# State-space stage of a decoder layer: the states of all pairs as one stream, four engines in program order

## The chip, the cores and the metric

The kernel runs on one core of a Trainium2 chip. The time is device microseconds of one execution. The core's engines work side by side: PE (TensorE, matmuls, with its weight loads as PEld), DVE (VectorE), ACT (ScalarE), POOL (GpSimd) and SP (SyncE, which here only starts transfers). Each works through its own queue in order and waits on semaphores for the others.

## The reference, cut to what matters

A decoder layer on x of shape 8 x 256 x 128: a state-space (Mamba-like) block, a cross attention to a context, and six layers of windowed attention and gated feed-forward. Only the first is concerned. For D = 256 channels, N = 16 states and 4 convolution taps it computes:

```python
Xn = layernorm(X)
X_main = silu(causal_conv(Xn @ W_up1))                  # 256 channels
delta, Bm, Cm = split(X_main @ W_ll + b_ll)             # 256, 16, 16; softplus on delta
A_bar = exp(delta * A)                                  # per channel and state
U = X_main * (A_bar - 1) / (delta * A) * (delta * Bm)
H = A_bar[t] * H + U[t]                                 # scan over t
Y[t] = sum over n of Cm[t, n] * H[:, n]
out = X + (Y * silu(Xn @ W_up2)) @ W_down
```

Since (A_bar − 1) / (delta A) × delta Bm = (A_bar − 1) Bm / A, the kernel keeps w = X_main Bm / A and scans m = (m + dw) × A_bar with dw the difference of w in time; the rest of H is w itself, and its share of Y comes from one product over all states (`s_ps`, `xs`).

## The kernel before, in words

Two sequences make a pair; there are four pairs. Channels lie on partitions in two halves `h` of 128, the 512 columns are the pair's tokens. A unit is one state `n` of one half:

- VectorE: `wz` = xm × (1/A) × the broadcast row of B (L542), then two scans `m`, one per sequence (L523);
- POOL: `dw` = the time difference of `wz` (L548), and `mc` = m × the broadcast row of C (L525);
- ACT: `ab` = exp(A × dt) into PSUM (L98 is the line of a helper that many activations share);
- PE: the add of `mc` into `y` in PSUM with an identity matrix (L503);
- SP: per state two transfers `rows` of 256 KB that spread a row of B and one of C over the partitions (L537), read back from `bc_dram`, which ACT's queue wrote (L402).

Buffers: `rows` 4, `wz` 4, `dw` 3, `m` 2, `mc` 6, `ab` 2, and two small PSUM banks under the tag `s` that nearly every matmul other than `y` goes through. The scan of a unit is written two units behind its `wz`.

`scan` runs the 16 states of a pair. Between states it advances two generators by one step or two: `post`, which ends the pair before (gate `yg`, down projection `dn_ps`, layer norm, `x1`), and `pre`, which prepares the next pair (load and turn the tokens, statistics `bn_st` and `bn_mv`, turn again, `conv`, the activation into `xm`, the product `bc_ps` for B and C, `dt` by a softplus, and the gates). `xm` is copied to PSUM (`xm_ps`, L511) for states 2 and later; the first two states read `xm` itself. `y` is begun after state 2 by `s_ps` and `xs` (L556 to L559), and the adds begin at state 4. Beside pair 2 and in pair 3, `project` makes the first pair's queries, keys and values for the cross attention; for pair 0 it goes through the small banks, each half of an accumulator left by ACT at once.

The order: up to the first pair's `dt`, PE, ACT and VectorE run as written (`manual_schedule`). From there to the end of the stage a scheduler chooses each engine's order among what the program's steps offer, by estimated costs. A few edges hold it: `behind_exps` puts some ACT work behind the last `ab`, and `with_table` puts exponentials and logarithms behind the load of their activation table. The later stages are not touched, except that `project` for later pairs is written without its case for the first.

Of the kernel before, what the change touches and what calls it, by code (L numbers as in the profile page):

```python
# [9 lines left out]
FP = mybir.dt.float32  # L10
# [4 lines left out]
P = 128  # L15
B, S, D = 8, 256, 128
NPAIR = B // 2
TP = 2 * S
# [31 lines left out]
def decoder_kernel(ctx: ExitStack, tc: tile.TileContext, a: dict, out: bass.AP):  # L50
# [163 lines left out]

    def project(p, got):
# [23 lines left out]
        got.update(qT=qT, kT=kT, v=v)  # L239
        for j in range(NHB // 2):  # L240
            for dst, w, src, q in ((qT, wq, la, True), (kT, wkv, cn, False)):
                pr = ps_big("pr") if big else None
                for i in range(2):
                    c = 2 * j + i
                    o = pr[:, i * TP : (i + 1) * TP] if big else ps_s("pr")
                    T.matmul(  # L246
                        o, lhsT=w[:, c * P : (c + 1) * P], rhs=src, start=True, stop=True
                    )
                    if not big:
                        A.activation(dst[:, c, :], o, AF.Copy, scale=HD**-0.5 if q else 1.0)  # L250
                d2 = dst[:, 2 * j : 2 * j + 2, :].rearrange("p c t -> p (c t)")
                if big and q:
                    A.activation(d2, pr, AF.Copy, scale=HD**-0.5)
                elif big:
                    V.tensor_copy(d2, pr)
                yield
        for j in range(4):
            pr = ps_big("pv") if big else None
            for i in range(2):
                at = slice(i * 512, (i + 1) * 512)  # L260
                o = pr[:, at] if big else ps_s("pv")
                T.matmul(
                    o, lhsT=cn[:, j * P : (j + 1) * P],
                    rhs=wkv[:, INNER + i * 512 : INNER + (i + 1) * 512], start=True, stop=True,
                )
                if not big:
                    A.copy(v[:, j, at], o)
            if big:
                A.copy(v[:, j, :], pr)
            yield  # L270


    with (
# [80 lines left out]
        def pre(p, got, t_in=None):  # L354
# [49 lines left out]
            got.update(bc=bc, cb=cb, b_ps=[])  # L404
# [26 lines left out]
            def minus_bc():  # L431

                c_ps = ps_s("c_ps")
                T.matmul(
                    c_ps[:NS], lhsT=ident[: 2 * NS, NS : 2 * NS], rhs=bc_sb, start=True, stop=True
                )
                V.scalar_tensor_tensor(cb, c_ps[:NS], -1.0, bc_sb[:NS], ALU.mult, ALU.mult)

            if p:
                minus_bc()  # L440
                for h in range(2):
                    d_ps = step_of(h)
                    yield
                    softplus(h, d_ps)
                yield
            else:

                for h in range(2):
                    d_ps = step_of(h)
                    t = ps1.tile([P, TP], FP, tag="ab", name="b_ps")  # L450
                    T.matmul(
                        t, lhsT=ident[: 2 * NS, h : h + 1].to_broadcast([2 * NS, P]), rhs=bc_sb,
                        start=True, stop=True,
                    )
                    got["b_ps"].append(t)
                    softplus(h, d_ps)
                yield
                minus_bc()
            g_ps = []
            for h in range(2):  # L460
                g_ps.append(ps_s("g_ps"))
                T.matmul(
                    g_ps[h], lhsT=w_up2[:, h * P : (h + 1) * P], rhs=xn, start=True, stop=True
                )
            yield
            load_table("exp_and_others")
            for h in range(2):
                g = sp.tile([P, TP], FP, tag=f"gate{h}", name="gate")
                with behind_exps():
                    with_table(A.activation, g, g_ps[h], AF.Tanh)  # L470
                V.scalar_tensor_tensor(g, g, 1.0, g_ps[h], ALU.add, ALU.mult)
                gate.append(g)
            load_table()
# [21 lines left out]
        def scan(p, x, xm, gate, dt, bc, b_ps, cb, steps, spare):  # L495


            y = [ps_o("y0"), ps_o("y1")]
            late = []

            def add_up():
                for h, n, mc in late:
                    T.matmul(y[h], lhsT=ident, rhs=mc, start=False, stop=(n == NS - 1))  # L503
                late.clear()

            xp1 = []
            for h in range(2):
                t = ps1.tile([P, TP], FP, tag=f"xm{h}", name="xm_ps", bufs=1)  # L510
                A.copy(t, xm[h])  # L511
                xp1.append(t)

            def scan_of(h, n, dw, rows):
                c = h * NS + n
                ab = ps1.tile([P, TP], FP, tag="ab", name="ab")
                exps.append(
                    with_table(A.activation, ab, dt[h], AF.Exp, scale=aa[:, c : c + 1])
                )
                m = sp.tile([P, TP], FP, name="m")  # L520
                for b in range(2):
                    t = slice(b * S, (b + 1) * S)
                    V.tensor_tensor_scan(m[:, t], dw[:, t], ab[:, t], 0.0, ALU.add, ALU.mult)  # L523
                mc = sp.tile([P, TP], FP, name="mc", bufs=6)
                G.tensor_tensor(mc, m, rows[:, 1, :], ALU.mult)  # L525
                late.append((h, n, mc))

            waiting = []
            for n in range(NS):
                if n > 3:  # L530
                    add_up()

                rows = sp.tile([P, 2, TP], FP, name="rows", bufs=4)
                early = n < len(b_ps)
                for i in range(1 if early else 0, 2):
                    r = i * NS + n
                    nc.sync.dma_start(out=rows[:, i, :], in_=bc[r : r + 1, :].to_broadcast([P, TP]))  # L537
                for h in range(2):
                    c = h * NS + n
                    w = wzs.pop(0)  # L540
                    wzs.append(w)
                    V.scalar_tensor_tensor(  # L542
                        w[:, :, 1:], two((xm if n < 2 else xp1)[h]), ia[:, c : c + 1],
                        two(b_ps[n] if early else rows[:, 0, :]),
                        ALU.mult, ALU.mult,
                    )
                    dw = sp.tile([P, TP], FP, name="dw", bufs=3)
                    G.tensor_tensor(two(dw), w[:, :, 1:], w[:, :, :S], ALU.subtract)  # L548
                    waiting.append((h, n, dw, rows))

                    if len(waiting) > 2:
                        scan_of(*waiting.pop(0))
                if n == 2:
                    for h in range(2):
                        s_ps = ps_s("s_ps")
                        T.matmul(s_ps, lhsT=iaT[:, h, :], rhs=cb, start=True, stop=True)  # L556
                        t = sp.tile([P, TP], FP, tag=f"yg{h}", name="xs1")
                        V.tensor_tensor(t, xm[h], s_ps, ALU.mult)
                        T.matmul(y[h], lhsT=ident, rhs=t, start=True, stop=False)  # L559
                for _ in range(0 if n == 0 else 2 if n <= 5 or p == NPAIR - 1 else 1):  # L560
                    next(steps, None)
                if n > 5:
                    next(spare, None)
            for args in waiting:
                scan_of(*args)
            add_up()
            for _ in steps:
                pass
            return y

        def both(*gens):

            gens = list(gens)
            while gens:
                for g in list(gens):
                    try:
                        next(g)
                    except StopIteration:
                        gens.remove(g)
                        continue  # L580
                    yield

        nxt = {}
        last = pre(0, nxt, t_in0)
        engines = {mybir.EngineType.PE, mybir.EngineType.Activation, mybir.EngineType.DVE}
# [9 lines left out]
        turn_decay()  # L595
        for p in range(NPAIR):
            cur, nxt = nxt, {}
            if p == 1:
                load2()
            if p == NPAIR - 2:  # L600
                beside = project(0, first)
            ahead = pre(p + 1, nxt) if p + 1 < NPAIR else beside
            y = scan(p, **cur, steps=both(last, ahead), spare=beside if p == NPAIR - 2 else iter(()))
            last = post(p, cur["x"], cur["gate"], y)
# [671 lines left out]
```

## Time and profile before

| what | value |
|---|---|
| runs | 2251.42, 2255.55, 2256.18 us; median 2255.55 |
| profiled execution | 2257.74 us, of which the span on the core is 2255.9 |
| state-space stage | first `dw` at 28.2 us, last `mc` ends at 375.2 |
| cross attention and the six layers | from about 376 us to the end |
| busy in the whole span | PE 2100.3, DVE 1734.9, ACT 1430.0, POOL 1637.5 us |

Busy time by stretch, from the windows view (us busy, instructions in brackets, granted TensorE clock as a share of full speed); the four stretches are roughly the four pairs:

| stretch, us | PE | DVE | ACT | POOL | clock |
|---|---|---|---|---|---|
| 28 to 110 | 63.95 (118) | 66.44 (113) | 44.28 (69) | 68.82 (62) | 0.82 |
| 110 to 185 | 57.15 (126) | 65.49 (112) | 35.77 (56) | 67.75 (60) | 0.83 |
| 185 to 275 | 69.61 (146) | 76.06 (124) | 46.79 (75) | 76.37 (67) | 0.81 |
| 275 to 376 | 80.42 (160) | 75.79 (118) | 40.91 (67) | 83.46 (74) | 0.88 |

In a line of the groups stand the source line, the engine, the operation, output <- inputs with shapes, the count, then busy us and mean ns of one, then the idle time of that engine just before these instructions and who ended it. In a line of a timeline stand start and duration in us, and in brackets the idle time before it and who ended it; neighbours of the same kind are merged into one line (x2, x4). Durations in the timeline overlap by some 0.05 us, so what an instruction costs its engine is read from start to start. The ends of matmuls are modelled; a 128x512 matmul in float32 shows as two instructions.

### The profile page before, as it was taken

The page shows a single profiled execution, that of the slowest core. Times are in us where ns is not written, and L with a number is a line of the kernel's source. Part 1 is how long each engine was busy: PE and PEld are TensorE (multiplying, and loading weights), DVE is VectorE, ACT ScalarE, POOL GpSimd, SP SyncE. Part 2 cuts the span into 40 slices and gives each one's busy share as a digit, 9 for nine tenths or more (in the row PEclk, how much of TensorE's full clock was granted, in tenths as well). Part 3 has the DMA queues.
Part 4 walks back from the last instruction along what each step waited for, and adds up shares of the span by engine and source line. Part 5 has one row for each costly group of instructions (what it writes and reads, how often), then busy time and mean ns, then how long its engine had stood idle before and what let it go on. Part 6 is the DMA issues. An engine that isn't in the chain of part 4 may idle for free.

```text
span 2255.9 us, 77045 instructions
## 1 busy us (share of the span) xinstructions
PE 2100.3 (93%) x32482; PEld 1314.6 (58%) x32482; DVE 1734.9 (77%) x2533; ACT 1430.0 (63%) x2438; POOL 1637.5 (73%) x1440
## 2 busy tenths in 40 slices
PE   7877888999988999999999999999999999999986
PEld 3232333444444776666767667676776767667653
DVE  6798876444366988888898888888888888888852
ACT  5544544555455777777667777777766677777644
POOL 4888887222267988888888888888888888888740
PEclk8887989999999999999999999999999999999998
DMA  4443331000203444434443434444443434333330
GB/s 138 97 105 95 98 94 47 6 5 1 64 25 58 71 71 85 76 71 78 75 86 70 77 67 87 76 77 70 76 85 68 78 66 83 68 67 65 62 58 10
DMA packets 438326, 155.41 MB, mean 69 GB/s; under 512 B 401886, under 2 KB 418140, under 8 KB 437852
## 3 DMA queue, kind: packets, MB, share of 16 engines
q1 hardware_dynamic: 437500, 150.10, 34.1%
q8 instruction: 255, 4.18, 0.8%
q14 instruction: 91, 0.75, 0.1%
q10 hardware_dynamic: 480, 0.38, 0.1%
HBM read 54.68 MB, written 1.31 MB: 25 GB/s over the span
## 4 chain that ended last, share of the span: by engine, by line
PE 70%; DVE 7%; ACT 6%; POOL 2%; issue 2%; DMA 0%; DVEq 0%; POOLq 0%; ACTq 0%
PE qk_ps L686 13%; PE y_ps L863 7%; PE qkT_ps L742 7%; PE o_ps L849 7%; PE f_ps L933 6%; PE v_ps L686 6%; PE s_ps L790 5%; PE pT_ps L832 3%; PE f_ps L961 3%; PE pr L246 3%; PE o_ps L1107 2%; PE s_ps L1088 2%; ACT ln_sq L98 1%; PE y_ps L1145 1%; DVE rb L704 1%
## 5 line engine op out<-in xcount | busy, mean ns | idle before, releaser
L707 POOL TENSOR_TENSOR qk<-qk,rb 128x512 f32<-128x512 f32 x384 | 481.0, 1274 | 48.4 <-DVE rb L704 29.6
L735 POOL TENSOR_TENSOR qk<-qk,rn 128x1024 f32<-128x1024 f32 x192 | 365.5, 1904 | 12.4 <-ACT rn L98 12.3
L686 PE MATMUL qk_ps<-wqkv,xs 128*128 128x512 f32 x768 | 363.9, 596 | 2.4 <-ACT kz L752 1.4
L812 POOL TENSOR_TENSOR pw<-pw,mx 128x512 f32<-128x512 f32 x192 | 202.0, 1052 | 168.1 <-DVE mx L811 167.9
L709 ACT ACTIVATE sq<-qk_ps 128x1024 f32<-128x1024 f32 x192 | 196.9, 1026 | 165.7 <-PE o_ps L849 123.1
L703 DVE TENSOR_TENSOR qk<-qk_ps,tab 128x1024 f32<-128x1024 f32 x192 | 228.8, 1192 | 67.1 <-PE qk_ps L686 66.2
L704 DVE TENSOR_TENSOR rb<-qk_ps,tab 128x1024 f32<-128x1024 f32 x192 | 233.1, 1214 | 0.0
L716 DVE TENSOR_REDUCE ss<-sq 128x16 f32<-128x1024 f32 x192 | 229.1, 1193 | 5.1 <-ACT sq L709 5.0
L825 POOL TENSOR_TENSOR pw<-pw,mx 128x512 f32<-128x512 f32 x192 | 200.4, 1044 | 39.2 <-ACT fxn L920 32.0
L1097 POOL TENSOR_TENSOR ws<-w 128x512 f32<-128x512 f32 x64 | 81.5, 1273 | 195.7 <-ACT w L98 152.7
L863 PEld LDWEIGHTS y_ps<-oT,wo 128*128 128x128 f32 x1536 | 186.2, 192 | 46.6 <-issue 33.5
L742 PE MATMUL qkT_ps<-ident,qk 128*128 128x128 f32 x1536 | 209.5, 279 | 4.0 <-POOL qk L735 2.9
L525 POOL TENSOR_TENSOR mc<-m,rows 128x512 f32<-128x512 f32 x128 | 163.1, 1278 | 40.2 <-PE y L503 20.4
L863 PE MATMUL y_ps<-oT,wo 128*128 128x128 f32 x1536 | 187.5, 275 | 1.9 <-ACT pT L836 1.6
L857 DVE STREAM_TRANSPOSE oT<-o_ps 128x512 f32<-128x512 f32 x192 | 126.1, 695 | 82.0 <-PE o_ps L849 82.0
L686 PEld LDWEIGHTS qk_ps<-wqkv,xs 128*128 128x128 f32 x768 | 131.3, 191 | 97.5 <-issue 93.0
L523 DVE TENSOR_TENSOR_SCAN m<-dw,ab 128x256 f32<-128x256 f32 x256 | 159.8, 668 | 31.6 <-POOL mc L525 29.8
L790 PEld LDWEIGHTS s_ps<-kz,qT 64*32 64x32 f32 x12288 | 137.8, 105 | 76.1 <-issue 38.6
L686 PE MATMUL v_ps<-wqkv,xs 128*128 128x512 f32 x384 | 180.6, 592 | 0.3 <-ACT sq L709 0.3
L742 PEld LDWEIGHTS qkT_ps<-ident,qk 128*128 128x128 f32 x1536 | 165.2, 141 | 23.8 <-POOL qk L735 3.8
L98 ACT ACTIVATE ab<-dt,aa 128x512 f32<-128x512 f32 x128 | 87.6, 689 | 139.9 <-DVE m L523 136.5
L849 PE MATMUL o_ps<-vz,pT 64*32 64x64 f32 x12288 | 168.6, 225 | 2.3 <-issue 2.3
(187 smaller groups left out, 4146.7 us busy)
## 6 DMA issues: line engine op xcount, KB each, us to landing
vz<-v SPq DMA_DIRECT2D x1152, 64.0 KB, 2.2
rows<-bc_dram SPq DMA_DIRECT2D x126, 256.0 KB, 4.2
vz<-v SPq DMA_DIRECT2D x576, 32.0 KB, 2.0
wqkv<-in_L_ffn_Wqkv SPq DMA_DIRECT2D x18, 512.0 KB, 4.7
wo<-in_L_ffn_Wo SPq DMA_DIRECT2D x48, 64.0 KB, 2.4
w<-in_L_ffn_W SPq DMA_DIRECT2D x6, 341.0 KB, 3.4
t_in<-in_x SPq DMA_DIRECT2D x4, 256.0 KB, 3.4
wkv<-in_L_xattn_Wkv SPq DMA_DIRECT2D x1, 1024.0 KB, 8.0
```

The costliest lines, as they stand in the source:

```text
L686: T.matmul(pr[:, i * 512 : (i + 1) * 512], lhsT=got[n]["xs"][:, tb * P : (tb + 1) * P], rhs=thirds[seq[n][0], c][:, i * 512 : (i + 1) * 51 ...
L703: V.tensor_tensor(t, p3, cs, ALU.mult)
L704: V.tensor_tensor(rb, p3, sn, ALU.mult)
L707: G.tensor_tensor(t[:, :, o], t[:, :, o], rb[:, :, f], ALU.add)
L716: V.tensor_reduce(got[n]["ss"][:, 2 * c + tb, :], got[n]["sq"], AX.X, ALU.add)
L735: G.tensor_tensor(t, t, r, ALU.mult)
L742: T.transpose(t_ps[:, hb * P : (hb + 1) * P], t[:, 2 * hb : 2 * hb + 2, :].rearrange("p h d -> p (h d)"), ident,)
L790: T.matmul(s_ps[i * W : (i + 1) * W, e, c : c + 2 * W], lhsT=qT[r, 4 * g + i, j * W : (j + 1) * W], rhs=kz[r, 4 * g + i, k0 : k0 + 2 * W], ...
L812: G.tensor_tensor(pw, pw, mx[:, 0].unsqueeze(3).to_broadcast([P, 4, 2, 2 * W]), ALU.subtract)
L825: G.tensor_tensor(pw, pw, mx[:, 1].unsqueeze(3).to_broadcast([P, 4, 2, 2 * W]), ALU.mult)
L849: T.matmul(o_ps[i * W : (i + 1) * W, e, c : c + HD], lhsT=pT[r, j, i * W : (i + 1) * W], rhs=vz[r, j, i, :], start=True, stop=True, tile_p ...
L863: T.matmul(y_ps[:, :P], lhsT=wts[d][0][:, hb, :], rhs=got[n]["oT", wh][:, hb // 4, (hb // 2) % 2, :].rearrange("p (w h q) -> p h w q", w=4 ...
```

## The change

Program order now holds for PE, ACT, VectorE and POOL through the whole stage (`manual_schedule` over the four pairs, POOL added). The generators are gone. The states of all pairs form one stream: the units that wait for their scan, and the products that wait for their add, are carried over the border from one pair to the next. After each state `n` of pair `p`, `ended(p - 1, n)` does one step of ending the pair before (states 1 to 5) and `prepare(p + 1, n)` one step of the next pair's preparation (states 1 to 15). Gates and `dt` of a pair are complete before its first state; for pair 0 the gates come after states 1 to 3. `y` of a pair is begun in `ended` at state 2 (`start_y`), for pair 0 after state 1, and adds that have no `y` yet wait in a list. `ab` of the units that still wait is made ahead (`decay_of`). The next pair's activation table is changed once for `xm` and gates together (loads at states 7 and 12). `project` for the first pair is a function of its own: three matmuls a state, each left by ACT, and all of it beside pair 3.

The core of the diff (shortened; repeated parts of unchanged operations are left out):

```diff
+    def project_first(la, cn, qT, kT, v):
...
+        for i, (dst, w, src, scale) in enumerate(work):
+            if i % 3 == 0:
+                while out:
+                    leave()
+            if len(out) == 2:
+                leave()
+            o = ps_s("pr")
+            T.matmul(o, lhsT=w, rhs=src, start=True, stop=True)
+            out.append((dst, o, scale))
+            if i % 3 == 2:
+                yield
...
+        def prepare(p, c, n):
+            if n == 1:
+                c["t_in"] = load_x(p)
...
+            elif n == 3:
+                c["tp"] = turned_tokens(c["t_in"])
+            elif n == 4:
+                A.copy(c["x"], c["tp"])
...
+                for j in range(4):
+                    V.bn_stats(st[:, j, :], c["t_in"][:, j, :])
+                    V.bn_aggr(mv[:, j, :], st[:, j, :])
+            elif n == 5:
+                inv_root(rs, mv[:, :, 1], eps_t)
+                V.scalar_tensor_tensor(mv[:, :, 0], mv[:, :, 0], -1.0, rs, ALU.mult, ALU.mult)
...
+                c["tp"] = turned_tokens(t)
+            elif n == 6:
+                A.activation(xn, two(c["tp"]), AF.Identity, bias=col("ssm_b"), scale=col("ssm_g"))
+                c["acc"] = [ps_s("conv") for h in range(2)]
...
+            elif n in (7, 8, 9):
...
+            elif n == 10:
...
+            elif n == 11:
+                gate_tanhs(c)
+            elif n == 12:
+                gates(c)
+                load_table()
...
+                c["c_ps"] = minus_bc(c)
+                c["d_ps"] = dt_product(c, 0)
+            elif n == 13:
+                stored_bc(c, c["c_ps"])
+                c["ze"] = softplus(0, c["d_ps"])
+                c["d_ps"] = dt_product(c, 1)
+            elif n == 14:
+                dt_sum(c, 0)
+                c["ze"] = softplus(1, c["d_ps"])
+            elif n == 15:
+                dt_sum(c, 1)
...
+        def ended(p, c, n):
+            if n == 1:
...
+            elif n == 2:
+                A.activation(c["r"], c["dn"], AF.Identity, bias=col("ssm_bd"))
+                start_y(pairs[p + 1])
+                T.matmul(c["ln"], lhsT=mean_w, rhs=c["r"], start=True, stop=True)
...
+        def scan_next():
+            i = waiting.pop(0)
+            decay_of(i)
...
+        def start_y(c):
+            y = [ps_o("y0"), ps_o("y1")]
+            for h in range(2):
+                s_ps = ps_s("s_ps")
+                T.matmul(s_ps, lhsT=iaT[:, h, :], rhs=c["cb"], start=True, stop=True)
+                t = sp.tile([P, TP], FP, tag=f"yg{h}", name="xs1")
+                V.tensor_tensor(t, c["xm"][h], s_ps, ALU.mult)
+                T.matmul(y[h], lhsT=ident, rhs=t, start=True, stop=False)
+            c["y"] = y
+        def state(p, c, n):
+            add_up()
...
+                if len(waiting) > 2:
+                    scan_next()
+                if p or n > 1:
+                    for i in waiting:
+                        decay_of(i)
+        order1.enter_context(tc.manual_schedule(engines=engines))
         for p in range(NPAIR):
+            for n in range(NS):
+                state(p, c, n)
...
+                if p:
+                    ended(p - 1, pairs[p - 1], n)
+                if p < NPAIR - 1:
+                    prepare(p + 1, pairs[p + 1], n)
+                else:
+                    if n == 0:
+                        beside = project(0, first)
+                    if n == 1 or n > 2:
+                        next(beside, None)
```

## The prediction

> **What bounds the stage now.** The edit stays inside the state-space stage, so I read, in this order, the windows view (where the stage ends), the groups of POOL and VectorE in its window, and POOL's, VectorE's and PE's timelines there. A "unit" is one state of one half of the channels: one `wz`, one `dw`, two scans `m`, one `mc`; 4 pairs have 128.
>
> POOL's two groups over the first 377 us (count, busy us and mean ns, idle before and who ended it):
>
> ```profile
> L525 POOL TENSOR_TENSOR mc<-m,rows 128x512 f32<-128x512 f32 x128 | 163.1, 1278 | 40.2 <-PE y L503 20.4 <-issue 6.6 <-PE s_ps L556 5.3
> L548 POOL TENSOR_TENSOR dw<-wz 128x512 f32<-128x512 f32 x128 | 136.3, 1067 | 35.2 <-DVE wz L542 32.6 <-DVE m L523 2.4
> ```
>
> Every unit costs POOL a `dw` and an `mc`. In the timeline, POOL runs for long stretches without a gap and then stops dead, mostly on PE:
>
> ```profile
> 64.19 1.27 POOL L525 TENSOR_TENSOR mc<-m,rows 128x512 f32<-128x512 f32 x1 [8.29 <-PE y L503]
> ...
> 98.31 1.27 POOL L525 TENSOR_TENSOR mc<-m,rows 128x512 f32<-128x512 f32 x1
> 99.54 1.03 POOL L548 TENSOR_TENSOR dw<-wz 128x512 f32<-128x512 f32 x1
> 100.54 1.26 POOL L525 TENSOR_TENSOR mc<-m,rows 128x512 f32<-128x512 f32 x1
> ...
> 160.63 1.27 POOL L525 TENSOR_TENSOR mc<-m,rows 128x512 f32<-128x512 f32 x1 [3.49 <-PE bc_ps L393]
> ...
> 190.44 1.26 POOL L525 TENSOR_TENSOR mc<-m,rows 128x512 f32<-128x512 f32 x1 [5.08 <-PE s_ps L556]
> ...
> 277.90 1.26 POOL L525 TENSOR_TENSOR mc<-m,rows 128x512 f32<-128x512 f32 x1 [5.82 <-issue]
> ```
>
> and once more, in pair 3:
>
> ```profile
> 317.20 2.49 POOL L525 TENSOR_TENSOR mc<-m,rows 128x512 f32<-128x512 f32 x2 [7.38 <-PE y L503]
> ```
>
> From start to start a unit takes 100.54 − 98.31 = 2.23 us. The first `dw` starts at 28.2, the last `mc` ends at 375.2: 347.0 us. POOL's own work is 128 × 2.23 + 6 `dt` sums × 1.22 (start to start) = 292.8. So 54 us are lost; the five waits above are 30.1 of them, the rest lies in many gaps under 2 us. POOL is the floor, PE's and VectorE's order makes the gaps.
>
> VectorE in a calm stretch, then where `xm` comes from SBUF:
>
> ```profile
> 120.67 0.74 DVE L542 SCALAR_TENSOR_TENSOR wz<-xm_ps,ia,rows 128x512 f32<-128x512 f32 x1
> 121.32 1.25 DVE L523 TENSOR_TENSOR_SCAN m<-dw,ab 128x256 f32<-128x256 f32 x2
> 122.50 0.72 DVE L542 SCALAR_TENSOR_TENSOR wz<-xm_ps,ia,rows 128x512 f32<-128x512 f32 x1
> ```
>
> A unit costs VectorE 122.50 − 120.67 = 1.83 us, so per state (two units) it gains 2 × (2.23 − 1.83) = 0.80 us on POOL. That is what pays for everything else on VectorE.
>
> **The change, part by part.**
>
> *Lost waits.* The next pair's `bc`, `cb`, `dt` and gates are now finished at states 10 to 15 of the pair before, and `y` of a pair starts at its state 2 on PE with the four adds that are due right behind it, not behind a burst of other matmuls. In the built order of the changed kernel POOL alternates `dw`, `mc` across pair borders. I take all five big waits away (30.1 us) and then ask what is late next: VectorE, which now works in program order and waits at the heads of its queue for PE and ACT, with the scans and `wz` behind it, and POOL behind those.
>
> *The cushion.* `m` has two buffers: a scan starts when the `mc` two units back ends. From then POOL has four instructions before it needs the next state's `wz`: 2 × 2.23 = 4.46 us. Off go the scan (1.18), the `wz` (0.65) and some 0.3 for handovers: VectorE may lose 2.3 us at one place before POOL stands. A ledger for pair 1 or 2 starts with 2.3 and gains 0.80 per state.
>
> - States 0 and 1: four `wz` read `xm` and `rows`, both in SBUF. Their group has 17.6 us for 12, mean 1469 ns against 733 with `xm` in PSUM; from 109.69 to 119.48 the four units took 9.8 us, not 4 × 1.83 = 7.3, so 2.5 more. Left: 2.3 − 2.5 + 1.6 = 1.4. POOL's own instructions in that stretch are longer by 1.3 (an `mc` of 1.71 for 1.27, `dw` of 2.48 for two).
> - State 1 to 2: two `yg` (1.2), PE's three `dn`, `s_ps`, then `xs`, `y`, `s_ps`, `xs` in turn. Before, other work stood between. PE at this place is slow in the trace:
>
> ```profile
> 302.21 2.07 PE L556 MATMUL s_ps<-cb,iaT 16*128 16x512 f32 x2 [1.39 <-ACT qT L250]
> 304.21 2.08 PE L559 MATMUL y<-xs,ident 128*128 128x512 f32 x2
> 306.08 1.91 PE L487 MATMUL dn_ps<-yg,w_dn 128*128 128x512 f32 x2
> ...
> 310.57 1.02 PE L488 MATMUL dn_ps<-x,twice 128*128 128x512 f32 x2
> ```
>
>   A 128x512 matmul (two instructions) takes 1.7 to 1.9 us start to start at first and 0.86 some 8 us later. I count from the end of state 1's scans. The first `dn` starts at 0.75, behind one `yg`; with three matmuls at 1.75 and the rest at 0.9 the first `s_ps` ends at 6.9, `xs` at 7.6, `y` and `s_ps` at 9.5, the second `xs` at 10.2. Without all this VectorE would be through state 2 at 2 × 1.83 = 3.6. So 6.6 lost, 0.8 gained, 1.4 in hand: POOL stands 4.4 us. With all at 0.9 it is 2.2, with all at 1.75 it is 6.9; three is what the trace has in the bursts from 211.7 and 302.2 on (three to four).
> - State 3: `ln_xc` 0.6, covered. State 4: four `bn_st` and `bn_mv`, 1.45 (three and four of them took 1.0 from 270.9 on): 0.45 uncovered. State 5: `x` 0.6, then `bn_mv` waits for ACT's two small `ln_rs` behind an `ab` (0.65 + 0.5 + 0.1) and takes 0.6: 1.9, 1.1 uncovered.
> - States 8, 9, 12, 13 (`xm`, gates, `cb`: 3.1) lie in 8 us of gained time: nothing.
>
> Pair 1 or 2: 32 × 2.23 + 2.44 = 73.8, plus 1.3 + 4.4 + 0.45 + 1.1 = 81.1.
> Pair 0 has the `s_ps`/`y` chain at state 1 with no cushion: `cb` 0.6, `s_ps` 1.9, `xs` 0.6, `y` and `s_ps` 3.7, `xs` 0.6 from 33.0 on; the next `dw` at about 41.2 where POOL is idle from 35.5: 5.7. With 2.0 of first gaps as now and 1.3 at states 4 and 5: 82.8.
> Pair 3 runs the first projection instead. State 3 has `ln_xc`, statistics, a wait and four `t_in`: 4.4 − 0.8 = 3.6 uncovered; state 7 waits for two ACT roots behind an `ab` (2.0) and runs `la` twice (0.89 + 1.28): 4.1 − 0.8 − 1.2 in hand = 2.1. With 1.3 + 4.4: 71.4 + 11.4 = 82.8.
>
> Sum: 28.2 + 82.8 + 2 × 81.1 + 82.8 = 356 for the end of the last `mc`, now 375.2: 19 us.
>
> *Moved at no cost, with its cover.* `rows`: a buffer is free at the `mc` four states back; VectorE asks for the next one at the earliest two units and a scan later, 4.46 + 1.18 = 5.6 us, against 4.2 us (3.5 to 5.0) from issue to landing on SP's queue; if SP lets that margin slip, a wait like the 2.40 before the `wz` at 344.09 returns, once per slip. The `bc` store on ACT's queue now has five states before its first reader. ACT loses 6 of the stage's 18 table loads (1283 ns each) and is busy 36 to 47 us a pair: no gain, no loss. PE adds of one state wait behind the 8 `conv`: `mc` has six buffers, 13 us, against at most 12 at the slow rate. In pair 3, ten instructions a state × 0.43 = 4.3 us of 4.46; at the 0.88 clock of that quarter 4.9, up to 3.5 us late at the end of the stage, kept for the range. Behind the stage nothing moves.
>
> **A rule that speaks against it.** `s_ps` has a mean of 1026 ns and `y<-xs` 1100 where 592 is the fast figure, and the granted clock is 0.56 from 200 to 220 us, where PE only adds. "TensorE: Matmul & The Clock Gate" of the Trainium skill (Part 1) says that idling for about 3.4 us halves the clock and about as long of sustained work restores it; a PE that waits in order idles more. By that rule the burst would have two slow matmuls, not three, and the stall above 3.5 instead of 4.4.
>
> **Rivals.**
> 1. *The cushion does not work* (two `m` buffers, and the waits sit exactly where it is spent). Then all of VectorE's other work falls on POOL: `yg`, `xs` and their chain 6.6, `wz` 2.5 and POOL's 1.3, `ln_xc`, statistics, `x`, `bn_mv` 4.0, `xm`, gates, `cb` 3.1: 17.5 a pair, 73.8 + 17.5 = 91.3, four pairs and the start 393: 18 us slower, 2274. It decides from 347.0/4 − 73.2 = 13.5 us a pair on. For it: 44 scan waits for `mc` in the window show how short the leash is. Against: around 125 VectorE takes `xs` and `yg` and POOL goes on.
> 2. *VectorE's extras hide nearly wholly*, PE being busy enough to keep its clock: 28.2 + 292.8 = 321 at best, 54 us faster; half of my stalls gives 338, 37 faster: 2219, range 2201 to 2224. Against: the chain at state 2 is serial whatever the clock.
> 3. *PE becomes the bound.* Pair 1 has 114 long matmul instructions × 0.43 + 2 = 51 us at full clock; at 51/86.8 = 0.59 mean clock it takes as long as now. At 0.55: 93 us, the stage's end at 399, 24 slower, 2280. Clocks of 0.81 to 0.88 per pair speak against.
> 4. *No change beyond 0.2%*: new stalls eat the 54 by chance.
>
> **How the numbers follow.** The profiled execution took 2257.74 us (span 2255.9, 1.8 around it); the median of three runs is 2255.55, 2.2 lower. I forecast the median: 2255.55 − 19 = 2236. Unknowns of the forecast case: PE's rate (3 × 2.2 less or 3 × 2.5 more), pair 0 (3), pair 3 (4), `rows` slips (up to 5 × 2.4), PE's tail 3.5; not all at once: 2224 to 2252. Chances: forecast 0.60, rival 2 0.17, rival 1 0.12, rival 3 0.04, rival 4 0.07. The range takes the forecast case, the slower half of rival 2 and rival 4: 2212 to 2254, leaving out about 0.2. No change means within 0.2%, 4.5 us, about what runs of this kernel can tell (they lie 4.8 apart): faster 0.78, same 0.07, slower 0.15.
>
> **What would show it.** Right: the last `mc` ends near 356; POOL's waits for PE `y` at most a few us; gaps of 2 to 5 us at state 2 of each pair, ended by `wz` or scans, with VectorE's `xs` waiting for `s_ps`; `wz` waits for `rows` under 8 us in all. Wrong: POOL gaps in every state (rival 1), `mc` waiting for PE `y` in mid-pair (rival 3), an end before 340 (rival 2), or a stage behind 376 that is not as long as before.

## The result, and the profile after

| | before | after |
|---|---|---|
| median | 2254.70 us (5 runs, 2251.42 to 2256.18) | 2239.36 us (5 runs, 2236.05 to 2245.17) |
| ratio | | 0.9926, interval 0.9913 to 0.9939 |
| profiled execution, span | 2257.74, 2255.9 us | 2237.36, 2235.6 us |
| first `dw` to end of last `mc` | 25.22 to 375.2: 350.0 us | 25.22 to 358.40: 333.2 us |
| of it POOL waits (brackets of its timeline, summed) | 50.7 | 33.9 |
| behind the stage | 1880.7 | 1877.2 |

The kernel is 0.74% faster. The stage is 16.8 us shorter, and POOL's waits in it are 16.8 us fewer: the same work with fewer holes. The 3.5 us behind the stage are not counted as gain: that time lies anywhere from 1875.0 to 1886.0 us in the profiled executions of the experiments below, whose later stages all have the same text. The prediction counted from "the first `dw`" at 28.2; that is the third one, the first two start at 25.22 in both kernels, so no difference depends on it. Stage lengths below count from 25.22.

POOL's groups over the first 360 us (count, busy us and mean ns, idle before and who ended it), and VectorE's two `wz` forms:

```profile
L693 POOL TENSOR_TENSOR mc<-m,rows 128x512 f32<-128x512 f32 x128 | 166.7, 1303 | 3.5 <-DVE m L691 1.4 <-PE t_ps L166 0.4
L726 POOL TENSOR_TENSOR dw<-wz 128x512 f32<-128x512 f32 x128 | 133.9, 1046 | 56.1 <-DVE wz L721 56.1
```

```profile
L721 DVE SCALAR_TENSOR_TENSOR wz<-xm_ps,ia,rows 128x512 f32<-128x512 f32 x112 | 81.6, 729 | 0.0
L721 DVE SCALAR_TENSOR_TENSOR wz<-xm,ia,rows 128x512 f32<-128x512 f32 x12 | 30.2, 2520 | 0.0
L702 DVE TENSOR_TENSOR xs<-xm,s_ps 128x512 f32<-128x512 f32 x8 | 5.5, 687 | 18.8 <-PE s_ps L700 18.8
```

The 20.4 us that POOL's `mc` waited for PE's adds are gone, and every wait of weight now ends with a `wz` (24.0 of the 56.1 lie ahead of the first `dw`). `wz` never waits for `rows`; in the trace before it did so 15 times, 24.7 us in all, and how much of POOL's waits hung on that was not separated. What is new stands in the second line of VectorE: with both operands in SBUF a `wz` has a mean of 2520 ns, 1469 before.

POOL's timeline, the start of a pair's stall in each pair and, around 102 to 114, the border of pairs 0 and 1:

```profile
41.65 1.04 POOL L726 TENSOR_TENSOR dw<-wz 128x512 f32<-128x512 f32 x1 [7.73 <-DVE wz L721]
...
102.19 1.07 POOL L726 TENSOR_TENSOR dw<-wz 128x512 f32<-128x512 f32 x1
103.19 1.30 POOL L693 TENSOR_TENSOR mc<-m,rows 128x512 f32<-128x512 f32 x1
104.41 1.07 POOL L726 TENSOR_TENSOR dw<-wz 128x512 f32<-128x512 f32 x1
105.41 1.29 POOL L693 TENSOR_TENSOR mc<-m,rows 128x512 f32<-128x512 f32 x1
106.63 1.30 POOL L622 TENSOR_TENSOR dt<-z,ez 128x512 f32<-128x512 f32 x1
108.62 1.04 POOL L726 TENSOR_TENSOR dw<-wz 128x512 f32<-128x512 f32 x1 [0.69 <-DVE wz L721]
109.78 1.63 POOL L693 TENSOR_TENSOR mc<-m,rows 128x512 f32<-128x512 f32 x1
...
112.38 1.71 POOL L693 TENSOR_TENSOR mc<-m,rows 128x512 f32<-128x512 f32 x1
...
128.13 1.04 POOL L726 TENSOR_TENSOR dw<-wz 128x512 f32<-128x512 f32 x1 [4.70 <-DVE wz L721]
...
210.25 1.04 POOL L726 TENSOR_TENSOR dw<-wz 128x512 f32<-128x512 f32 x1 [4.55 <-DVE wz L721]
...
292.40 1.04 POOL L726 TENSOR_TENSOR dw<-wz 128x512 f32<-128x512 f32 x1 [4.32 <-DVE wz L721]
299.94 1.04 POOL L726 TENSOR_TENSOR dw<-wz 128x512 f32<-128x512 f32 x1 [2.89 <-DVE wz L721]
...
319.88 1.04 POOL L726 TENSOR_TENSOR dw<-wz 128x512 f32<-128x512 f32 x1 [1.95 <-DVE wz L721]
```

VectorE and PE around the border of pairs 0 and 1:

```profile
102.26 6.22 DVE L721 SCALAR_TENSOR_TENSOR wz<-xm,ia,rows 128x512 f32<-128x512 f32 x1
...
111.39 1.57 DVE L721 SCALAR_TENSOR_TENSOR wz<-xm,ia,rows 128x512 f32<-128x512 f32 x1
...
116.73 1.25 DVE L631 TENSOR_TENSOR yg<-y,gate 128x512 f32<-128x512 f32 x2
...
123.68 0.69 DVE L702 TENSOR_TENSOR xs<-xm,s_ps 128x512 f32<-128x512 f32 x1 [2.05 <-PE s_ps L700]
126.63 0.69 DVE L702 TENSOR_TENSOR xs<-xm,s_ps 128x512 f32<-128x512 f32 x1 [2.27 <-PE s_ps L700]
127.24 0.74 DVE L721 SCALAR_TENSOR_TENSOR wz<-xm_ps,ia,rows 128x512 f32<-128x512 f32 x1
```

```profile
117.48 3.75 PE L635 MATMUL dn_ps<-yg,w_dn 128*128 128x512 f32 x4 [1.28 <-issue]
121.03 1.56 PE L636 MATMUL dn_ps<-x,twice 128*128 128x512 f32 x2
122.52 1.12 PE L700 MATMUL s_ps<-cb,iaT 16*128 16x512 f32 x2
124.42 1.12 PE L703 MATMUL y<-xs,ident 128*128 128x512 f32 x2 [0.78 <-DVE xs L702]
```

Two things to read here. From 116.73 to 127.24, 10.5 us, VectorE does two units' work (3.6 us), the two `yg` and the two `xs`, and 4.32 us of it go into waiting, because each `xs` waits for a sum on PE; POOL stands 4.70 us at the end of it. And the first `wz` of the pair lasts 6.22 us: in that time POOL ran `dw`, `mc`, `dw`, `mc`, `dt` without a gap, and the `wz` ended at 108.48, only after POOL had run out of work at 107.9. The Trainium skill ("SBUF — State Buffer", section "SBUF: two separate sides") says that VectorE with two SBUF inputs and GpSimd share a port pair under an exclusive lock, held for a whole instruction. The trace agrees that one side blocks wholly, but here the loser waits for a whole row of instructions, not for one.

### The profile page after: what moved, and what is told of

Its sections match the earlier page's. It is cut to its first block, busy times and chain, and to the rows that moved or that the text cites. A ratio compares the mean times of both kernels' runs of the same rounds, so it can differ in the third digit from the quotient of the medians.

```text
span 2235.6 us, 77068 instructions
## 1 busy us (share of the span) xinstructions
PE 2096.8 (94%) x32482; PEld 1314.8 (59%) x32482; DVE 1743.8 (78%) x2533; ACT 1422.2 (64%) x2432; POOL 1636.2 (73%) x1440
## 4 chain that ended last, share of the span: by engine, by line
PE 73%; DVE 13%; ACT 7%; issue 4%; POOL 3%; DMA 0%; SPq 0%; DVEq 0%; POOLq 0%; ACTq 0%
PE qk_ps L875 13%; PE y_ps L1052 8%; PE qkT_ps L931 7%; PE o_ps L1038 7%; PE f_ps L1122 6%; PE v_ps L875 6%; PE s_ps L979 5%; DVE m L691 4%; PE pT_ps L1021 3%; PE f_ps L1150 3%; PE o_ps L1296 2%; PE pr L279 2%; PE s_ps L1277 2%; DVE wz L721 2%; ACT ln_sq L98 1%
## 5 line engine op out<-in xcount | busy, mean ns | idle before, releaser
L1286 POOL TENSOR_TENSOR ws<-w 128x512 f32<-128x512 f32 x64 | 81.4, 1272 | 196.8 <-ACT w L98 154.1
L979 PEld LDWEIGHTS s_ps<-kz,qT 64*32 64x32 f32 x12288 | 138.2, 105 | 74.5 <-issue 33.4
L726 POOL TENSOR_TENSOR dw<-wz 128x512 f32<-128x512 f32 x128 | 133.9, 1046 | 56.1 <-DVE wz L721 56.1
L691 DVE TENSOR_TENSOR_SCAN m<-dw,ab 128x256 f32<-128x256 f32 x256 | 160.9, 669 | 12.8 <-POOL mc L693 11.4
```

Source lines behind the costliest of these rows:

```text
L691: V.tensor_tensor_scan(m[:, t], i["dw"][:, t], i["ab"][:, t], 0.0, ALU.add, ALU.mult)
L979: T.matmul(s_ps[i * W : (i + 1) * W, e, c : c + 2 * W], lhsT=qT[r, 4 * g + i, j * W : (j + 1) * W], rhs=kz[r, 4 * g + i, k0 : k0 + 2 * W], ...
```

## Experiments

Three questions were open. Which half of the change brought the gain: steps spread over the states, or the program order? What makes the stall at state 2: order, PE's clock, or an empty cushion? What does the 6.22 us `wz` cost? My theory: POOL is the floor, and what is left of its waits is VectorE blocked in its order, by the chain of state 2 and by the `wz` from SBUF. The rivals are in the expectations. Each kernel is the changed one with the edit shown.

All results; "stage" is from the first `dw` to the end of the last `mc`, "waits" the sum of POOL's waits in it, "work" the rest. The stage figures come from one profiled execution each. The ratio is to runs of the kernel before that were taken beside each kernel; their median was 2252.36 to 2254.70 us, so medians of different rows can be a microsecond or two off against each other.

| kernel | stage, us | against after | waits | work | median, us | ratio (interval) |
|---|---|---|---|---|---|---|
| before | 350.0 | +16.8 | 50.7 | 299.3 | 2254.70 | 1 |
| after | 333.2 | 0 | 33.9 | 299.3 | 2239.36 | 0.9926 (0.9913–0.9939) |
| e12_burst | 346.8 | +13.6 | 49.7 | 297.1 | 2251.35 | 0.9994 (0.9984–1.0004) |
| e6_scheduler | 317.6 | −15.6 | 19.6 | 298.0 | 2224.18 | 0.9866 (0.9850–0.9882) |
| e7_pool_free | 332.8 | −0.4 | 33.2 | 299.6 | 2239.43 | 0.9936 (0.9923–0.9949) |
| e1_two_sums_first | 326.9 | −6.3 | 27.6 | 299.3 | 2233.44 | 0.9920 (0.9907–0.9933) |
| e2_sums_ahead | 318.1 | −15.1 | 19.2 | 298.9 | 2223.79 | 0.9876 (0.9863–0.9889) |
| e5_pe_warm | 329.8 | −3.4 | 30.1 | 299.7 | 2234.15 | 0.9911 (0.9896–0.9925) |
| e3_xm_copied_ahead | 322.4 | −10.8 | 27.5 | 294.9 | 2226.78 | 0.9886 (0.9870–0.9902) |
| e4_m_three | 332.8 | −0.4 | 33.7 | 299.1 | 2239.85 | 0.9945 (0.9933–0.9957) |
| e8_xm_m | 320.6 | −12.6 | 25.7 | 294.9 | 2225.32 | 0.9877 (0.9864–0.9891) |
| e10_xm_sbuf | 376.6 | +43.4 | 33.9 | 342.7 | 2280.61 (one run) | |
| e9_all | 308.1 | −25.1 | 14.0 | 294.1 | 2213.19 | 0.9825 (0.9811–0.9838) |
| e13_all_scheduler | 303.4 | −29.8 | 10.2 | 293.2 | 2214.14 | 0.9822 (0.9809–0.9836) |

### Which half of the change

**e12_burst** undoes the spreading of the last six preparation steps.

```diff
-                    prepare(p + 1, pairs[p + 1], n)
+                    for k in (n,) if n < 10 else range(10, NS) if n == NS - 1 else ():
+                        prepare(p + 1, pairs[p + 1], k)
```

> One part of the change undone: the preparation steps of states 10 to 15 (bc and its store, gate products and tanhs, gates, cb, dt products, softplus, dt sums) are all done in one piece behind state 15, in program order; the rest stays. My theory: the border of a pair then has a chain that no cushion of 2.3 us covers: ACT runs bc 0.6, two table loads 2.6, two tanhs 1.4 and eight softplus passes 5.2 (9.8 us), VectorE's gates and cb wait for it and the next wz stand behind them, the rows of the next pair are loaded only behind the store (over 4.2 us); POOL stands 6 to 10 us at each of three borders: the last mc ends 18 to 30 us after 358.4, at 376 to 388, which is what the kernel before had (375.2) or worse. Rival (the cushion and the other half's work hide it): under 6 us.

POOL's timeline of this kernel at the first border:

```profile
111.31 1.38 POOL L622 TENSOR_TENSOR dt<-z,ez 128x512 f32<-128x512 f32 x1 [6.10 <-ACT ez L98]
114.67 1.26 POOL L622 TENSOR_TENSOR dt<-z,ez 128x512 f32<-128x512 f32 x1 [1.98 <-ACT ez L98]
```

The stall at a border is the one expected (6.10 + 1.98 = 8.1 us, 23.0 over three), but the end was only 13.6 later, where I gave 18 at least. While POOL stands there, VectorE gets ahead: the stalls at state 2 fall to 2.50, 2.12 and 3.38 (5.6 less in all) and the `wz` from SBUF fall in part where POOL stands (mean 1050 ns). So a new wait pays part of the next one. With that, the kernel cannot be told from the one before: under the fixed order, four fifths of the gain (13.6 of 16.8) hang on spreading six steps.

**e6_scheduler** keeps the spreading and gives the order back.

```diff
-        order1.enter_context(tc.manual_schedule(engines=engines))
```

> The text of the changed kernel with its order over the stage given back to the scheduler, which may move instructions on PE, ACT, VectorE and POOL; one half of the change alone (steps spread over the states, without the fixed program order). If the spreading of the next pair's preparation brings the gain, the last mc ends within 6 us of 358.4, and POOL's waits for PE y (20.4 before) stay near nothing. If the program order brings it, PE's and VectorE's queues are shuffled again, waits for PE come back, and the end goes to 365 to 378, the time to 2246 to 2258. I lean to the first, two to one; the scheduler may also start the sums of the next pair ahead by itself, which would give what the experiment with the sums ahead gave (15 us less).

```profile
L693 POOL TENSOR_TENSOR mc<-m,rows 128x512 f32<-128x512 f32 x128 | 166.6, 1302 | 9.1 <-DVE m L691 3.8 <-issue 2.4 <-PE ln_mu L642 2.1
L726 POOL TENSOR_TENSOR dw<-wz 128x512 f32<-128x512 f32 x128 | 133.8, 1046 | 34.6 <-DVE wz L721 34.1 <-DVE bn_mv L176 0.5
```

These are POOL's groups: 23.4 of the 34.1 lie ahead of the first `dw`. The waits for PE's adds did not return, and the stage is 15.6 us shorter than in program order; I had this only as an aside. In pair 1 the scheduler issues both sums of state 2 together, and VectorE takes a `wz` at 117.78 between the `xs` at 117.17 and 118.44:

```profile
115.69 2.31 PE L700 MATMUL s_ps<-cb,iaT 16*128 16x512 f32 x4
...
117.78 0.74 DVE L721 SCALAR_TENSOR_TENSOR wz<-xm_ps,ia,rows 128x512 f32<-128x512 f32 x1
```

The stalls there are 2.40, 2.18 and 2.01 (each with a later wait of 0.7), and pair 0's 7.73 becomes 2.36. So everything in the change but the fixed order gives 32.4 us (350.0 to 317.6), and the program order takes 15.6 of them back. That everything is the spreading together with the one stream over the borders, `ab` made ahead and the projection's own function. e12 says that the spreading weighs most, but it says so under the fixed order; without the order, the parts were not tried apart.

**e7_pool_free** frees POOL alone.

```diff
-        order1.enter_context(tc.manual_schedule(engines=engines))
+        order1.enter_context(tc.manual_schedule(engines=engines - {mybir.EngineType.Pool}))
```

> POOL alone is given back to the scheduler; PE, VectorE and ACT keep program order. In the built order POOL then has the two dt sums of a pair some units away from where they stand in program order, and nothing else is moved. My theory (POOL is limited by how early wz come, and its own order only matters where it waits for a z of ACT): the last mc ends within 2 us of 358.4 if the sums are taken later, or a few us later if a sum stands at POOL's head before ACT has its z and ez: up to 2 us a sum, 6 sums, 12 us at most. Rival (POOL's order is what the change gains by): 10 us or more lost.

Nothing (−0.4 us): POOL's own order is not what costs; the waits sit on VectorE's side.

### The stall at state 2

**e1_two_sums_first**

```diff
+            s_ps = [ps_s("s_ps"), ps_s("s_ps")]
+            for h in range(2):
+                T.matmul(s_ps[h], lhsT=iaT[:, h, :], rhs=c["cb"], start=True, stop=True)
             for h in range(2):
...
-                V.tensor_tensor(t, c["xm"][h], s_ps, ALU.mult)
-                T.matmul(y[h], lhsT=ident, rhs=t, start=True, stop=False)
+                V.tensor_tensor(t, c["xm"][h], s_ps[h], ALU.mult)
+                xs.append(t)
+            for h in range(2):
+                T.matmul(y[h], lhsT=ident, rhs=xs[h], start=True, stop=False)
```

> The chain at the head of a pair has both s_ps matmuls first, then both xs, then both y; in the changed kernel VectorE's second xs waits for an s_ps that stands behind a y that waits for the first xs. My theory (POOL is the floor, and it stands where VectorE is blocked in order by this chain): the second xs comes one y and one handover earlier, 1.12 + 0.8 = 1.9 us in pairs 1 to 3, 3.1 us in pair 0 where all four matmuls are slow (2.04 + 0.8, rounded up for a second handover); POOL's waits for wz fall from 7.73, 4.70, 4.55, 4.32 to about 4.6, 2.8, 2.6, 2.4, and the last mc ends 8 to 9 us before 358.4, at about 350. Rival (the cushion is too short and whatever VectorE saves is spent elsewhere): under 3 us. Rival (PE's slow clock decides, not the order): the slow matmuls stay as they are and the wait only moves to the other xs, under 2 us.

The stalls became 4.58, 2.75, 3.60 and 3.71: 6.3 us, not 8 to 9. Pair 0 gave its 3.1. In pairs 1 to 3 the second `xs` follows the first after 1.90 us instead of 2.95, 1.05 less, not 1.9: in this trace the second sum still starts behind the first `xs` (0.78 us after PE was free). Why it waits was not tried; in e6 the second sum starts right behind the first. The rest is the clock: pair 1's three `dn` matmuls were 0.9 us shorter than in the changed kernel (granted clock over them 0.66 for 0.54), pair 3's 0.5 longer (0.54 for 0.59).

**e2_sums_ahead** makes the sums and `xs` of pairs 1 to 3 beside states 14 and 15 of the pair before.

```diff
             elif n == 14:
+                state_sum(c, 0)
                 dt_sum(c, 0)
...
             elif n == 15:
+                state_sum(c, 1)
                 dt_sum(c, 1)
```

> The two s_ps matmuls and xs of the next pair are done beside states 14 and 15 of the pair before (for pairs 1 to 3; pair 0 stays as it is), so that at state 2 only the two y matmuls are left, for which VectorE does not wait. My theory: POOL's waits of 4.70, 4.55 and 4.32 at state 2 of pairs 1 to 3 go (13.6), the small ones behind them at states 4 and 5 too, since the cushion is no longer spent there (0.3 + 0.8 in pairs 1 and 2, some 1 to 2 of pair 3's 4.8); the last mc ends 14 to 18 us earlier, near 342. Pair 0's wait of 7.73 stays. Rival (the SBUF-SBUF wz at states 0 and 1 eat the cushion, and the chain is only where it shows): the waits move to states 1 and 3, and under 7 us are gained.

As expected: the stalls of 4.70, 4.55 and 4.32 are gone, those of 0.32 with them; 15.1 us. Only 0.83 is left in mid-pair in pairs 1 and 2, and a 0.41 in pair 2. The `wz` from SBUF still make POOL wait at the heads of the pairs (0.70, 0.69 and, in pair 3, 1.40 us), though the longest now takes 3.20 and 3.67 us in pairs 1 and 2; so they do not by themselves make POOL stand at state 2.

**e5_pe_warm** adds three matmuls that nothing reads at states 14, 15, 0 and 1.

```diff
+            if (p < NPAIR - 1 and n > 13) or (p and n < 2):
+                wt = ps_s("warm")
+                for _ in range(3):
+                    T.matmul(wt, lhsT=ident, rhs=c["xm"][0], start=True, stop=True)
```

> Three extra 128x512 matmuls of the identity with xm, whose result nobody reads, stand in PE's queue at each of the states 14, 15, 0 and 1 around a pair border, so that PE is not idle before the chain of state 2. Nothing else changes; pair 0's chain has none ahead of it. Theory of the clock (the chain's first two to three matmuls are slow because PE has been idle): dn, s_ps and y run at 0.86 to 1.0 us each; the chain ends 2 x 0.9 to 2.5 x 0.9 = 1.8 to 2.3 us earlier a pair, POOL's waits of 4.70, 4.55, 4.32 become 2.4 to 2.9, and the last mc ends 5 to 7 us before 358.4. Rival (the chain is a matter of order and handovers, and the extra matmuls only stand before s_ps): no gain, or a loss of up to 3 x 0.9 a pair.

```profile
115.04 2.74 PE L712 MATMUL warm<-xm,ident 128*128 128x512 f32 x6
117.61 1.88 PE L635 MATMUL dn_ps<-yg,w_dn 128*128 128x512 f32 x4
119.33 1.02 PE L636 MATMUL dn_ps<-x,twice 128*128 128x512 f32 x2
```

PE's timeline at pair 1: start to start the three `dn` take 2.67 us, 5.04 in the changed kernel (granted clock 1.00 for 0.54), and POOL's stall falls from 4.70 to 2.53. Pair 2 gives 1.70. Pair 3 gives 0.11: there the extra matmuls were themselves slow (3.86 us for three) and stood in front of `dn`. So the clock is nearly half of the stall in pair 1 and less in pair 2; what is left belongs to the order, and e2 takes both.

### The `wz` from SBUF and the cushion

**e3_xm_copied_ahead**

```diff
-                    w[:, :, 1:], two((c["xm"] if n < 2 else c["xp1"])[h]), ia[:, o : o + 1],
+                    w[:, :, 1:], two((c["xm"] if n < 2 and not p else c["xp1"])[h]), ia[:, o : o + 1],
...
+                if n == NS - 1 and p < NPAIR - 1:
+                    t = ps1.tile([P, TP], FP, tag=f"xm{h}", name="xm_ps", bufs=1)
+                    A.copy(t, pairs[p + 1]["xm"][h])
+                    pairs[p + 1].setdefault("xp1", []).append(t)
...
-                if n == 0:
+                if n == 0 and not p:
```

> At state 15 ACT copies the next pair's xm to PSUM, and states 0 and 1 of pairs 1 to 3 read it there, as all other states do; pair 0 stays as it is. So no wz of pairs 1 to 3 has both operands in SBUF. My theory: the wz of 6.22 us at the head of a pair goes back to about 0.73, POOL's waits of 0.69 to 0.70 there go, and its mc stay at 1.27 to 1.30 instead of 1.63 to 1.71: 2.2 us a pair on POOL; and VectorE comes to the chain of state 2 with its whole cushion, 1 to 2 us more of the 4.5 us stalls: 3 to 4 us a pair, 9 to 12 in all, the last mc near 348. Rival (the long wz is only time in which VectorE would have waited for m's buffers anyway, so the lock costs what POOL's own instructions lose): 3 to 6 us in all. Rival (ACT's two extra copies delay ab or x at the border): nothing or a loss.

10.8 us. POOL's work falls by 4.4 us (mean `mc` 1272 ns for 1303), its 0.7 at the pairs' heads go, and the stalls at state 2 become 3.42, 2.05 and 3.54, 4.6 less together. So the `wz` from SBUF cost POOL twice: its own instructions take longer beside them, and VectorE comes to the chain with less in hand.

**e4_m_three**

```diff
-            m = sp.tile([P, TP], FP, name="m")
+            m = sp.tile([P, TP], FP, name="m", bufs=3)
...
```

> m gets a third buffer (xm, which is read far ahead, one instead of two, to make room). Theory of the simple cushion: VectorE may run one unit further ahead, 2.23 us more at every place where it is blocked; POOL's waits of 4.7, 4.55, 4.32 and 7.73 fall by up to 2.2 each, pair 3's 2.89 and 1.95 go: 8 to 13 us. Theory of the lock: the first wz of a pair waits until POOL has nothing left to do, whatever the cushion; with a third buffer it waits one unit longer (about 8.4 us for 6.22), the cushion is empty all the same at state 1, and the stalls at state 2 stay within 0.5 us; only pair 3's later ones shrink: 0 to 4 us.

VectorE's timeline:

```profile
101.52 7.26 DVE L721 SCALAR_TENSOR_TENSOR wz<-xm,ia,rows 128x512 f32<-128x512 f32 x1
```

The `wz` began earlier against POOL and lasted 7.26 us, 1.04 more; it ended at 108.78, again just before the `dw` that POOL was waiting with (108.93). The stall at state 2 is 4.69 where it was 4.70. Whatever lead VectorE brings to the head of a pair, it loses there. The cushion's size is not the limit at state 2 as long as that `wz` stands. Pair 0's 7.73 and pair 3's 2.88 and 1.95 stayed as well, where the lock theory let pair 3's shrink; this run does not say why.

**e8_xm_m** has both edits.

> Both single edits at once: next pair's xm copied to PSUM ahead (alone: last mc at 347.1) and m with a third buffer (alone: 358.4, no gain). Theory of the lock (the third buffer bought nothing because the first wz of a pair waits until POOL is dry, however far ahead VectorE was): with no such wz the third buffer gives VectorE 2.23 us more at each later block, so POOL's 3.42, 2.05 and 3.54 at state 2 become 1.2, 0 and 1.3, pair 3's 2.89 and 1.94 become 0.7 or less, the small ones of states 4 and 5 go: 8 to 12 us on top, the last mc at 335 to 339, time near 2216. Rival (the cushion was never the limit, both edits are what they are alone): 347 again, within 2 us.

A miss: 1.8 us on top of e3, not 8 to 12. VectorE at the border, first e3_xm_copied_ahead, then e8_xm_m:

```profile
100.52 1.26 DVE L691 TENSOR_TENSOR_SCAN m<-dw,ab 128x256 f32<-128x256 f32 x2 [0.32 <-POOL mc L693]
104.12 0.75 DVE L721 SCALAR_TENSOR_TENSOR wz<-xm_ps,ia,rows 128x512 f32<-128x512 f32 x1 [2.34 <-ACT xm_ps L727]
```

```profile
99.44 1.26 DVE L691 TENSOR_TENSOR_SCAN m<-dw,ab 128x256 f32<-128x256 f32 x2 [0.32 <-POOL dw L730]
104.27 0.75 DVE L721 SCALAR_TENSOR_TENSOR wz<-xm_ps,ia,rows 128x512 f32<-128x512 f32 x1 [3.56 <-ACT xm_ps L727]
```

Two reasons. In a calm stretch a scan waits 0.32 us either way, for `mc` with two buffers, for `dw` with three: it needs the `dw` that it reads, so the third buffer was worth one `mc`, about 1.2 us of lead, not 2.23. And at the border that lead goes into the wait for ACT's copy, 3.56 for 2.34, 1.22 more. The copy stands in ACT's queue behind a `z` that waits for POOL's `dt` sum (2.94 us in e3, 4.16 here). My edit had put a new block in the place of the old one.

**e10_xm_sbuf** lets every `wz` with `rows` read `xm` in SBUF.

```diff
-                    w[:, :, 1:], two((c["xm"] if n < 2 else c["xp1"])[h]), ia[:, o : o + 1],
+                    w[:, :, 1:], two(c["xm"][h]), ia[:, o : o + 1],
```

> Nearly the opposite of copying xm ahead: every wz reads xm in SBUF, in all states and pairs, not in the first two alone, beside rows in SBUF. If the price is that of states 0 and 1 of a pair in the changed kernel (POOL's mc 1.71 for 1.27, start to start 2.67 for 2.23 once it is under way): 120 units more x 0.44 = 53 us, less what of the stalls at state 2 falls away: the last mc at 395 to 412. If VectorE is held at every wz until POOL has nothing to do, as by the first wz of a pair: POOL's whole unit of 2.23 and a wz of 0.72 one behind the other, 2.95 and more: 128 x 0.72 = 92 more, 440 to 460. If the long wz is only a wait for buffers that the trace draws so: 358.

The last `mc` ends at 401.2, the stage is 43.4 longer. POOL's waits are the same 33.9; its work grew from 299.3 to 342.7, by a mean `mc` of 1517 ns (1303), `dw` of 1142 (1046) and `dt` of 1483 (1290): (0.214 + 0.096) × 128 + 6 × 0.193 = 40.8 of the 43.4. So under way both sides lose a little at each unit, as the first of the three cases had it; no `wz` of this kernel lasts over 2 us. VectorE never gets far ahead here (its scans wait 5.4 us for `mc`, 11.4 in after). The blocks of 6 and 7 us were seen only where VectorE came with its lead and POOL had several instructions ready in a row.

### All together

**e9_all** is e2, e3 and e4 in one, and in pair 0 both sums come before the first `xs`, as in e1. The expectation says that they are made at state 0; in the kernel they stand behind state 1, where they stood.

> Everything that paid, in program order: sums of the next pair ahead at states 14 and 15, xm copied to PSUM ahead, m with three buffers, and in pair 0 both sums made at state 0, before the gates' products. If POOL's work of 128 x 2.23 + 6 x 1.22 = 292.8 us is the floor and all that is left are the start (25.2, first gaps 2) and some of pair 0's 7.7 and of pair 3's 4.8: the last mc ends at 325 to 332, 26 to 33 us before 358.4, time 2207 to 2214. If a new wait appears (ACT with the copies and the decays at a border, or the sums before the wz of states 14 and 15): 335 to 343, as with the sums ahead alone.

**e13_all_scheduler** is e9_all without the fixed order.

> The same text with its order given back to the scheduler on PE, ACT, VectorE and POOL. With the waits already taken out of program order the scheduler has less to win than the 16 us that it won on the changed kernel: the last mc within 5 us of that of the kernel in program order, either way. Rival (the scheduler's order is better by itself, by what it puts between waits): again 10 us or more ahead. Rival (it moves steps of the next pair ahead of wz, or splits a table load): behind by 5 to 15 us.

e9_all ends its stage at 333.3, between the two cases that I gave, 25.1 us shorter than after. The parts alone, e2 15.1, e3 10.8 and pair 0's 3.1, less the 4.6 at state 2 that e2 and e3 both count, make 24.4. POOL's work is 294.1, near the 292.8 of the prediction, and 14.0 us of waits are left: 4.58 in pair 0, 1.66 and 1.88 in pair 3, small ones. Its median of 2213.19 is 1.75% under the kernel before, where the changed one was 0.74% under it: 23 us between the two by these ratios, 26 by the medians. With the waits out of the way the scheduler gains 4.7 us in the stage (15.6 on the changed kernel) and has the same time: behind the stage its profiled execution takes 1886.0 us, e9_all's 1875.0. Some of these 11.0 us are scatter, for the profiled execution of e13 is the slowest of its four (2215.80, median 2214.14) and that of e9 the fastest of its five (2210.07, median 2213.19). On the clock its stage ends 5.2 us earlier (328.0 for 333.3), but POOL's first instruction of the next stage starts only 2.5 us earlier (339.26 for 341.75); where the rest goes stays open.

## Why the prediction held

The forecast was 2236 us in 2212 to 2254, faster by more than 0.2% with a chance of 0.78; measured were 2239.36 and 0.74%. Its own steps:

| step | predicted | measured |
|---|---|---|
| big waits on PE | all go | all gone |
| pair 0, next `dw` behind the chain | 41.2, after 5.7 | 41.65, after 7.73 |
| stall at state 2, pairs 1 to 3 | 4.4 | 4.70, 4.55, 4.32 |
| states 4 and 5 | 0.45, 1.1 | 0.32, 0.82 |
| pair 3, states 3 and 7 | 3.6, 2.1 | 2.89, 1.95 |
| states 0 and 1, POOL | 1.3 | 0.69 wait + 1.24 longer `mc` |
| pairs 0 to 3, from the third `dw` | 82.8, 81.1, 81.1, 82.8 | 80.4, 82.3, 82.4, 85.1 |
| end of the last `mc` | 356 | 358.40 |
| `wz` waits for `rows` | under 8 | 0 |

**The chain** was counted well: first `s_ps` done 6.9 us behind the scans (6.91 in the trace), second `xs` done at 10.2 (10.5). In pair 0 the chain ended where I put it, 0.45 us late; POOL had run dry earlier, so the wait is longer and the gaps ahead of it shorter. **PE's slow matmuls.** In the trace the two `dn` from `yg` take 1.78 us each and the third 1.49, 1.29 and 1.06 in pairs 1 to 3. With 1.75 for a slow one and 0.86 for a fast one, pair 1 has nearly my three slow ones, pair 3 nearer the two that I had worked out from the skill's rule ("TensorE: Matmul & The Clock Gate", Part 1), and pair 2 lies between. The stall still came out within 0.3 of my 4.4, because the `s_ps` and `y` behind them, one at a time, take 1.05 to 1.12 us each where I had 0.9.

**The term that was mis-sized** is states 0 and 1. I took the mean of 1469 ns from the trace of before, where other waits had kept POOL and VectorE apart. With POOL running without gaps, the first `wz` was held for 6.22 us and POOL lost about 1.9 us a pair, not 1.3. That (0.6) and the stall at state 2 (0.2 to 0.3 longer), less 0.4 at states 4 and 5, are 0.4 to 0.5 of the 1.2 us by which pairs 1 and 2 are longer than forecast; the rest, some 0.7, is POOL's plain work, 74.5 us in pair 1 where I had 73.8. That VectorE came out of it with 1.4 us in hand, as my ledger said (10.5 − 3.6 − 0.8 − 4.7), is by chance: e4 shows that the lead it brings to that `wz` makes no difference. In pair 3 the two `mc` that trail behind the last state add 2.5 us, which I had left in pair 0.

**Rivals.** The cushion that does not work (2274) is refuted as a whole, since the extras of states 8 to 13 cost nothing; but it has a true core, in that the cushion is empty at the head of each pair. Extras that hide (2219) fail on the chain. PE never became the bound: granted clock 0.79 to 0.87 by pair, no `mc` waiting for an add. **What I did not ask** is whether the fixed order is needed. I priced it as the source of the gain and of the new waits alike; e6 gives up the order alone and e12 part of the spreading alone; giving up both at once was not run.

## What to carry to other kernels

When a change both spreads work and fixes an order, try each alone: here the change without its order was worth 32.4 us of stage, and the order gave 15.6 of them back. In a fixed order look for a chain between two engines that alternate; make its first half a few steps ahead rather than hurrying it. A second buffer or a third helps only if nothing empties the lead just before it is needed, so follow the lead from place to place, and ask of every edit which queue it stands in.

## What the hardware showed beside

The `wz` with two SBUF inputs, 0.72 us at its shortest beside POOL, lasted 6.22 us, and 7.26 in e4, while POOL worked without a gap, and ended only when POOL ran dry: 0.55 us after the end of POOL's last instruction (107.92 and 108.47; in e4 108.23 and 108.78). With shorter rows of POOL's instructions it was 5.00 us in e7 and 3.20 in e2, and again it ended 0.55 us after the row. A few units later the same instruction took 1.57 us and POOL's next `mc` 1.71 for 1.27: there the two take turns, and the `wz` ends 0.55 us after the end of the one `dw` beside it (112.41 and 112.96). With one operand in PSUM (e3) there is none of it: no `wz` from SBUF is left in pairs 1 to 3, and POOL's mean `mc` is 1272 ns for 1303. What decides between the two was not found.
